# A cross-interaction network on one core: first tiles of three blocks by plain transfers, and a new order of fc's products, V2's spreading, loads of x and output transfers

## The chip, the core and the metric

The kernel runs on one core of a Trainium2 chip. A core has five engines, each with its own in-order queue of instructions: TensorE (PE in the profile; PEld is its loading of weights), VectorE (DVE), ScalarE (ACT), GpSimd (POOL) and SyncE (SP). Transfers between the chip's memory and the core's are issued by SP, ACT or POOL. The metric is the device time of one execution in microseconds (us), the median of several runs. Before the change it is 735.69 us, the median of three runs from 734.51 to 737.69.

## The reference

Inputs are x (1024 x 39 x 64: batch, fields F, embedding E), three weight matrices and the final layer. All is float32.

```python
def _cin_layer(Xk, X0, W, b):          # O = 64
    Wr = W.reshape(O, Hk, Fdim)
    return jnp.einsum('bhe,bfe,ohf->boe', Xk, X0, Wr) + b[None, :, None]
X0 = sparse_embedding; Xk = X0; outs = []
for W, b in ((W0, b0), (W1, b1), (W2, b2)):
    Xk = _cin_layer(Xk, X0, W, b)
    outs.append(Xk.sum(axis=-1))
return jnp.concatenate(outs, axis=-1) @ fc_w.T + fc_b
```

The last two layers are followed by nothing but sums and the final dot product, so their weights can be folded with fc_w. What is left per (batch, embedding) column is two quadratic forms of the 39 fields with 64 rows each: the first layer's, and one with W1 folded with "V2" (W2 folded with fc_w). They are multiplied with each other row by row, and summed.

## The kernel before, in words

**Work.** The 1024 x 64 columns are cut into 32 blocks of 2048 columns (`BLK`). The table `xd` in the chip's memory holds the fields as rows (39, and a row of ones): three buffers of two blocks each, filled by `load(n)`, a transfer of 1248 pieces of 256 bytes. A quadratic form needs the products of all pairs of fields. For blocks 0 to 3 and 30, 31 (the "whole" blocks) five tiles of 128 x 2048 (`rt[..][:, i]`, i = 0 to 4) are filled with rows of `xd` in five different orders (`label(i, row)`), so that the products of six pairs of tiles (`PAIRS`: (0,1), (0,2), (3,1), (3,2), (0,4), (3,4)), with one small product for two blocks, hold each pair of fields once. VectorE makes the products (`product`, L200), TensorE multiplies them with the weights `wa` (L551, four matmuls of 512 columns per product). The 26 blocks in between are done in another way (narrow lists, products at L736, matmuls at L763), which the change does not touch.

**Who fills the tiles.** `roll(n)` (L155) issues five indirect transfers from POOL, one per tile, each with a list of row numbers; `roll_small` fills two smaller tiles u and v. For block 0 the tiles are filled in two halves of 1024 columns from `xh`, two early copies of the first block (L370 to L376). Block n+2 uses block n's buffers: its transfers wait until the last product of block n that reads the tile. So blocks 0 to 3 are fetched while block 0 and 1 are computed.

**Start.** Before the first real matmul the weights have to be prepared, on TensorE with other engines in between (L254 to L500). In order: products without use (`spin`, L257, into a bank `idle` that nobody reads) keep TensorE busy. `turn` (L306) turns a row of fc_w into a column: a matmul with one contracted row and one output column. VectorE puts the column of fc's third part into `fc2` (L346). Four matmuls with `fc2` fold W2 (L386). `turn_twice` (L311, called at L394) turns fc's second part. VectorE transposes the folded W2 (`blocks`, L406). `spread_v2` (L420) doubles its rows, and VectorE masks it into `v2` (L433). `turn_w0` (L399) transposes W0 in seven pieces. Four matmuls with `v2` fold W1 (L467). VectorE (L480) and ScalarE (L444, L487, L490) put both into the table `both`, from which the pairs' weights are gathered (L508, L510), transposed (L527) and copied to `wa` (L528, L529). Then L551 begins.

**Order of the work after that.** It is written out: a list `steps`; `whole_step` multiplies step `at`, and `make` makes the product four steps ahead (`AHEAD`). Transfers stand where these functions issue them. On SP's queue are the row of ones for the second buffer (L349), the loads of x (L140), the rearranged weights `wn` (L700) and the fields for the finish (L793); on POOL's the rolls. At the end `y` (three rows of 256 results, L1081) leaves by SP's queue, and `yl` (the last 256, L1091) by ACT's.

```python
def turn(dst, row):
    nc.tensor.matmul(dst, row, one, start=True, stop=True)
...
def roll(n, tiles=range(NT), product=None):
    for i in tiles:
        k = n % 2 * NT + i
        gather_rows(tiles_of(n)[:, i], xd[n // 2 % NTAB][: FT if k < NT else 2 * FT], k, product)
```

Of the kernel before, what the change touches and what calls it, by code (L numbers as in the profile page):

```python
# [60 lines left out]
def label(i, row):  # L61
    if row < K:
        return (row % F + BASE[i] + STEP[i] * (row // F)) % F
    e = row - K
    if i == NT - 1 and e < ONLY:
        return F
    return 3 * e + (e >= ONLY) + (e > ONLY) + OFFSET[i]


# [45 lines left out]
def cin_kernel(ctx: ExitStack, tc: tile.TileContext, x, w0t, b0, w1, b1, w2, b2, fc_w, fc_b, out):  # L115
# [39 lines left out]
    def roll(n, tiles=range(NT), product=None):  # L155
        for i in tiles:
            k = n % 2 * NT + i
            gather_rows(tiles_of(n)[:, i], xd[n // 2 % NTAB][: FT if k < NT else 2 * FT], k, product)

    def roll_small(n):  # L160
        table = xd[n // 2 % NTAB].rearrange("f (t c) -> (f t) c", c=SUB)
        for k, dst in enumerate((ut, vt)):
            gather_rows(dst[n // 2 % 2], table, 2 * NT + k)
# [28 lines left out]
    unit = const.tile([128, 128], F32, name="unit")  # L192

    def product(n, c, cols=slice(0, BLK), p=None):
        if p is None:
            p = prods.tile([128, BLK], F32, name="p", tag="p")
        if c < NPAIR:
            i, k = PAIRS[c]
            r = tiles_of(n)
            nc.vector.tensor_tensor(p[:, cols], r[:, i, cols], r[:, k, cols], ALU.mult)  # L200
        else:
            nc.vector.tensor_tensor(p[:, 0:SUB], ut[n // 2 % 2], vt[n // 2 % 2], ALU.mult)
        return p

    prep = tc.tile_pool(name="prep", bufs=1)
    with prep as prep:
# [90 lines left out]
        for k, by in enumerate((*SHIFT, ROWS, *(ROWS + by for by in SHIFT[NK - 1 :]))):  # L297
            nc.gpsimd.memset(shift_of[:, k : k + 1], float(by))
        one = ones[0:1, 0, 0:1]

        def double(dst, src):
# [3 lines left out]
        def turn(dst, row):  # L305
            nc.tensor.matmul(dst, row, one, start=True, stop=True)  # L306
# [3 lines left out]

        def turn_twice(at, row, k):  # L311
            turn(small[:, at : at + 1], row[:, k].rearrange("p h s -> p (h s)"))

# [8 lines left out]
        first = pw[1][:, MM - 1 : MM]  # L322
        turn(first, fcrow2[:, 1].rearrange("p h s -> p (h s)"))
        spin(1, MM // 4)

# [44 lines left out]
        for k, cols in enumerate(halves):  # L370
            for i in range(4):
                gather_rows(rt[0][:, i, cols], xh[k], i)
                if k and i == 1:
                    load(1, nc.gpsimd)
        for k in (1, 0):
# [17 lines left out]

        turn_twice(6, fcrow2, 0)  # L394
        spin(1, 3 * MM // 8)

        def turn_w0(k):
# [5 lines left out]
            )  # L403

        for k in range(2):
            nc.vector.transpose(  # L406
                blocks[:, k].rearrange("p (f h) -> p f h", h=32),
                pv[k][:, 0:320].rearrange("p (h f) -> p f h", f=10),
            )
        nc.vector.tensor_scalar(v2v[:, 0, :, F - 32], mask, small[:, 6:7], None, ALU.mult)  # L410
        nc.vector.tensor_tensor(steps_at, steps_at, steps_by, ALU.mult)
# [16 lines left out]
        spread_v2(0, 0, 20)  # L428
        spread_v2(1, 1, 19)
        for k in range(7):  # L430
            turn_w0(k)
# [22 lines left out]
        roll_small(0)  # L454
        roll(1)
        for h in (0, H):
            nc.gpsimd.dma_start(b0s[h : h + H], b0.rearrange("(h o) -> h o", o=1))
        nc.gpsimd.dma_start(b1s, b1.rearrange("(h o) -> h o", o=1).to_broadcast([H, 2]))
        nc.gpsimd.dma_start(b2s, b2.rearrange("(h o) -> h o", o=1))
# [462 lines left out]
    for at, (n, c) in enumerate(steps[:3]):  # L922
        if at < 2:
            weight_rows(steps[3][1], slice(6 * at, 6 + 6 * at))
        product(n, c, halves[1], p[n, c])
    weight_rows(steps[4][1])
    n, c = steps[3]
# [15 lines left out]
    def whole_step(at, n, c):  # L943
        if at == NPAIR - 1:
            nc.scalar.copy(ones1, ones)
            fill_ones(1, nc.sync, ones1)
            for k in (2, 3):
                load(k)
        if (n, c) in ((0, NPAIR - 1), (2, 0)):
            load(2 * n + 4 - n // 2 * 2)  # L950
            load(2 * n + 5 - n // 2 * 2)
        quarters = range(BLK // MM)
# [40 lines left out]
    def make(at):  # L993
        step = steps[at]
        if len(step) == 2:
            n, c = step
            if NK < at <= NPAIR:
                weight_rows(c)
            p[n, c] = product(n, c)
            if c == NPAIR - 1 and n < 2:  # L1000
                rolls_due.append(lambda: roll(n + 2))
                if not n:
                    rolls_due.append(lambda: roll_small(2))
            if (n, c) == (2, NPAIR - 1):
                rolls_due.append(lambda: gather_slots(first_part, *range(7)))
            return
# [73 lines left out]
    nc.scalar.activation(y, py[0 : NY * 32, 0:YB], AF.Identity, bias=kfin)  # L1080
    nc.sync.dma_start(outv[0:NY], y[0 : NY * 32 : 32])  # L1081
    for lo, hi in ((0, done), (done, YB)):
# [6 lines left out]
        else:  # L1089
            nc.vector.tensor_scalar(yl[:, lo:hi], py, kfin[0:1], None, ALU.add)  # L1090
    nc.scalar.dma_start(outv[NY : NY + 1], yl)  # L1091

# [41 lines left out]
```

## Time and profile before

| | us |
|---|---|
| median of three runs (lowest, highest) | 735.69 (734.51, 737.69) |
| the profiled execution's own time | 737.69 |
| its span, from the first to the last instruction | 735.9 |
| TensorE busy (share of the span) | 728.6 (99%) |
| VectorE busy | 636.8 (87%) |
| POOL busy | 537.2 (73%) |
| ScalarE busy | 114.6 (16%) |
| bytes moved by all transfers | 153.56 MB, mean 209 GB/s |
| mean granted TensorE clock, share of full | 0.998 |

The profile shows one execution. Its own time is the highest of the three runs, and 1.79 us of it lie outside the span. In the chain of waits each row is a start, a length and what filled it; "issue" is time for which the profile shows no cause. In the timeline each row is a start, a length, engine, line, operation, and what is written from what; x4 says that four instructions stand in the row, and square brackets tell the idle time of the engine just before and who ended it. A float32 matmul is shown as two instructions. The profile's ends of matmuls are modelled.

### The profile page before, as it was taken

The numbers are of one execution on the slowest core, as the hardware profiler recorded it, in microseconds if no ns is written. First come the engines' busy times: TensorE is split into PE (matmuls) and PEld (weight loads), VectorE is DVE, ScalarE is ACT, GpSimd is POOL, SyncE is SP. The second block draws the span as 40 slices with busy tenths as digits, with TensorE's granted clock in tenths as the row PEclk, the third lists the DMA queues.
The fourth block names the chain that finished last, engine by engine and source line by source line (L and its number), as shares of the span: only waits on it lengthen the run. The fifth ranks groups of instructions, "written<-read, shape, count | busy, mean of one in ns | idle before, by whom it ended". The sixth has DMA issues, their size and how long they took to land.

```text
span 735.9 us, 13756 instructions
## 1 busy us (share of the span) xinstructions
PE 728.6 (99%) x5930; PEld 339.0 (46%) x5930; DVE 636.8 (87%) x558; ACT 114.6 (16%) x198; POOL 537.2 (73%) x292
## 2 busy tenths in 40 slices
PE   8999999999999999999999999999999999999998
PEld 5444444444444444444444444444444444444443
DVE  6997999688897988979888897988979888897996
ACT  3242210020200202011020200202011020200322
POOL 7758988649778696987869778696987869775200
PEclk9999999999999999999999999999999999999999
DMA  9889998843938558284673937558294673855600
GB/s 299 306 262 411 374 293 254 260 153 96 319 94 250 195 159 293 68 299 141 201 245 93 321 94 253 193 157 289 70 301 142 206 240 95 288 175 190 268 1 0
DMA packets 77363, 153.56 MB, mean 209 GB/s; under 512 B 43848, under 2 KB 43917, under 8 KB 73974
## 3 DMA queue, kind: packets, MB, share of 16 engines
q0 software_dynamic: 32304, 130.39, 50.0%
q1 hardware_dynamic: 43298, 20.30, 11.3%
q10 hardware_dynamic: 1700, 1.99, 0.9%
q8 instruction: 46, 0.75, 0.4%
q14 instruction: 15, 0.12, 0.1%
HBM read 150.54 MB, written 10.60 MB: 219 GB/s over the span
## 4 chain that ended last, share of the span: by engine, by line
PE 98%; another core or an unknown queue 0%; issue 0%; DVE 0%; ACT 0%; DVEq 0%; ACTq 0%
PE po L763 76%; PE po L551 17%; PE po L776 2%; PE po L571 1%; PE idle L259 1%; PE po L582 0%; PE pv L386 0%; PE pw L399 0%; DVE flat L480 0%; ACT both L487 0%; PE tr L527 0%; DVE g L827 0%; PE po L691 0%; DVE sums L859 0%
## 5 line engine op out<-in xcount | busy, mean ns | idle before, releaser
L763 PE MATMUL po<-p,wc 32*128 32x512 f32 x1300 | 561.9, 588 | 0.0
L763 PE MATMUL po<-p,wn 32*128 32x512 f32 x3900 | 561.7, 588 | 0.0
L719 POOL DMA_INDIRECT r<-xd,narrow x130 | 381.0, 2931 | 99.0 <-DVE p L736 66.7
L763 PEld LDWEIGHTS po<-p,wn 32*128 32x128 f32 x3900 | 260.7, 185 | 209.8 <-issue 209.6
L763 PEld LDWEIGHTS po<-p,wc 32*128 32x128 f32 x1300 | 239.4, 185 | 86.6 <-issue 82.1
L736 DVE TENSOR_TENSOR p<-r 128x2048 f32<-128x2048 f32 x78 | 176.1, 2283 | 8.2 <-PE po L763 7.8
L825 ACT ACTIVATE z<-po,columns 64x512 f32<-64x512 f32 x128 | 87.3, 682 | 544.2 <-PE po L763 504.0
L736 DVE TENSOR_TENSOR p<-r,u 128x2048 f32<-128x2048 f32 x52 | 118.7, 2282 | 15.5 <-DMA r<-xd,narrow 8.0
L551 PE MATMUL po<-p,wa 128*128 128x512 f32 x288 | 127.5, 600 | 1.8 <-ACT wa L528 1.8
L200 DVE TENSOR_TENSOR p<-r 128x2048 f32<-128x2048 f32 (+2 forms) x42 | 82.1, 1978 | 8.2 <-DMA r<-xd,lists 5.1
L551 PEld LDWEIGHTS po<-p,wa 128*128 128x128 f32 x288 | 54.3, 192 | 70.8 <-issue 64.1
L147 POOL DMA_INDIRECT r<-xd,lists x26 | 67.5, 2594 | 25.9 <-DVE p L736 11.6
L736 DVE TENSOR_TENSOR p<-r,v 128x2048 f32<-128x2048 f32 x26 | 59.7, 2296 | 25.7 <-PE po L763 25.7
L827 DVE SCALAR_TENSOR_TENSOR g<-po,b0s,z 64x512 f32<-64x512 f32 x76 | 56.9, 749 | 5.7 <-ACT z L825 3.5
L719 POOL DMA_INDIRECT v<-xd,narrow x26 | 37.2, 1431 | 7.9 <-issue 7.9
L827 DVE SCALAR_TENSOR_TENSOR pairs<-po,b0s,z 64x512 f32<-64x512 f32 x26 | 19.5, 749 | 23.9 <-ACT z L825 21.7
L719 POOL DMA_INDIRECT u<-xd,narrow x26 | 27.5, 1057 | 7.9 <-issue 4.0
L809 DVE TENSOR_REDUCE sums<-g 103x16 f32<-103x1024 f32 x26 | 31.3, 1205 | 0.0
L827 DVE SCALAR_TENSOR_TENSOR both<-po,b0s,z 64x512 f32<-64x512 f32 x26 | 19.5, 749 | 0.8
L820 ACT COPY g<-r 39x1024 f32<-39x1024 f32 x12 | 12.1, 1042 | 31.9 <-DVE sums L848 18.9
L730 DVE TENSOR_TENSOR p<-u,v 128x1024 f32<-128x1024 f32 x13 | 15.7, 1209 | 1.1 <-PE po L763 1.1
L809 DVE TENSOR_REDUCE sums<-both 103x16 f32<-103x1024 f32 x13 | 15.7, 1205 | 0.0
(140 smaller groups left out, 184.4 us busy)
## 6 DMA issues: line engine op xcount, KB each, us to landing
xd<-in_x SPq DMA_DIRECT2D x30, 312.0 KB
g<-xd SPq DMA_DIRECT2D x26, 156.0 KB
r<-xd,narrow POOLq DMA_INDIRECT x130
pairs<-xd SPq DMA_DIRECT2D x13, 156.0 KB
both<-xd SPq DMA_DIRECT2D x13, 156.0 KB
wn<-wc SPq DMA_DIRECT2D x12, 168.0 KB
w2s<-in_w ACTq DMA_DIRECT2D x1, 624.0 KB
w1s<-in_w ACTq DMA_DIRECT2D x1, 624.0 KB
```

Source lines behind the costliest of these rows:

```text
L147: work = nc.gpsimd.indirect_dma_start(dst, None, table, bass.IndirectOffsetOnAxis(ap=lists[:, k : k + 1], axis=0))
L200: nc.vector.tensor_tensor(p[:, cols], r[:, i, cols], r[:, k, cols], ALU.mult)
L551: nc.tensor.matmul(po[n][m], wa[:, c, side : side + 2 * H], p[:, bass.ts(m, MM)], start=n % 2 == 0 and c == 0, stop=n % 2 == 1 and c == NP ...
L719: work = nc.gpsimd.indirect_dma_start(slot(k, j), None, table, bass.IndirectOffsetOnAxis(ap=narrow[:, j : j + 1], axis=0),)
L730: done = nc.vector.tensor_tensor(p[:, 0:SUB], slot(k, LEFT), slot(k, RIGHT + NK), ALU.mult)
L736: done = nc.vector.tensor_tensor(p.rearrange("p (k c) -> p k c", k=NK), slots(k, many, NK, side), slot(k, one)[:, bass.ts(side, MM)].unsqu ...
L763: nc.tensor.matmul(po[2 * k + side][s], weights(c, s)[:, kind : kind + 2 * H], p[rows, bass.ts(u, MM)], start=begin, stop=last and u == le ...
L776: nc.tensor.matmul(po[2 * k + side][s][half : half + H], weights(LINEAR, s)[:, H : 2 * H], slot(k, NK)[rows, bass.ts(side, MM)], start=Fal ...
L809: nc.vector.tensor_reduce(sums[:, at : at + BB].rearrange("p (h s b) -> p h s b", h=2, s=2)[:, :, side], g[k, side, b].rearrange("p (h b e ...
L820: nc.scalar.copy(gt[H : H + F], tiles_of(n)[0:F, 0, bass.ts(m, SUB)])
L825: nc.scalar.activation(z[one], po[n][m][other], AF.Identity, bias=fc0s[other])
L827: return lambda: nc.vector.scalar_tensor_tensor(gt[0:H, at], po[n][m][one], b0s[one], z[one], ALU.add, ALU.mult)
```

## The change

It does eight things, all outside the repeated middle of the kernel.

- `turn_wide` takes the place of `turn_twice`, and does the turn of fc's third part as well: it multiplies with a row of 128 ones (`line`) instead of one, and so writes 128 equal columns, of which the last is used. Both turns now stand ahead of the fold of W2, followed by a spin of 64 columns (128 before).
- Behind the fold of W2 stands a spin of 128 columns (a turn and a spin of 192 before).
- Behind `spread_v2` stand two new spins of 160 columns, ahead of `turn_w0`.
- `load(1)` on POOL's queue moves ahead of the four second-half gathers of block 0 (it stood between the second and the third).
- Tiles 0 and 1 of blocks 1, 2 and 3 no longer come by POOL's indirect transfers. `roll_plain` writes them by plain transfers on SP's queue, one per run of rows whose numbers go up in equal steps: 13 transfers for the two tiles. For block 1 they wait for the product of block 0's second step, second half.
- `load(2)`, `load(3)` move from SP's queue (where they followed the row of ones) to POOL's, behind block 1's tiles.
- `load(4)`, `load(5)` move from SP's queue to POOL's, ahead of block 3's tiles.
- At the end `y` leaves by ACT's queue and `yl` by SP's.

```diff
+def stretches(i):
+    found, row = [], 0
+    while row < 128:
+        first, n, by = label(i, row), 1, 0
+        if row + 1 < 128 and label(i, row + 1) > first:
+            by = label(i, row + 1) - first
+            while row + n < 128 and label(i, row + n) - label(i, row + n - 1) == by:
+                n += 1
+        if n > 16 and not any(n % k == 0 for k in range(7, 17)):
+            n -= n % 13
+        found.append((row, n, first, by))
+        row += n
+    return found
...
+    def roll_plain(n, i, product=None):
+        table = xd[n // 2 % NTAB][n % 2 * FT : n % 2 * FT + FT]
+        for row, many, first, by in stretches(i):
+            src = table[first : first + (many - 1) * by + 1 : max(by, 1)]
+            behind(nc.sync.dma_start(tiles_of(n)[row : row + many, i], src), product)
...
-        def turn_twice(at, row, k):
-            turn(small[:, at : at + 1], row[:, k].rearrange("p h s -> p (h s)"))
+        def turn_wide(dst, k):
+            row = fcrow2[:, k].rearrange("p h s -> p (h s)")
+            nc.tensor.matmul(dst, row, line, start=True, stop=True)
...
         first = pw[1][:, MM - 1 : MM]
-        turn(first, fcrow2[:, 1].rearrange("p h s -> p (h s)"))
-        spin(1, MM // 4)
+        turn_wide(pw[1][:, MM - MM // 4 : MM], 1)
+        second = small[:, MM - 1 : MM]
+        turn_wide(small[:, MM - MM // 4 : MM], 0)
+        spin(1, MM // 8)
...
                 gather_rows(rt[0][:, i, cols], xh[k], i)
-                if k and i == 1:
-                    load(1, nc.gpsimd)
+            if not k:
+                load(1, nc.gpsimd)
...
-        turn_twice(6, fcrow2, 0)
-        spin(1, 3 * MM // 8)
...
+        spin(1, MM // 4)
...
         spread_v2(1, 1, 19)
+        spin(2, 5 * MM // 16)
...
-        roll(1)
+        roll(1, range(2, NT))
...
+            for k in (2, 3):
+                load(k, nc.gpsimd)
...
+        if at == 1:
+            for i in range(2):
+                roll_plain(1, i, made[n, c])
...
-            for k in (2, 3):
-                load(k)
-        if (n, c) in ((0, NPAIR - 1), (2, 0)):
-            load(2 * n + 4 - n // 2 * 2)
-            load(2 * n + 5 - n // 2 * 2)
+        if (n, c) == (2, 0):
+            load(6)
+            load(7)
...
-                rolls_due.append(lambda: roll(n + 2))
+                for i in range(2):
+                    rolls_due.append(lambda i=i: roll_plain(n + 2, i))
+                rolls_due.append(lambda: roll(n + 2, range(2, NT)))
...
+                    for k in (4, 5):
+                        rolls_due.append(lambda k=k: load(k, nc.gpsimd))
...
-    nc.sync.dma_start(outv[0:NY], y[0 : NY * 32 : 32])
...
-    nc.scalar.dma_start(outv[NY : NY + 1], yl)
+    nc.sync.dma_start(outv[NY : NY + 1], yl)
+    nc.scalar.dma_start(outv[0:NY], y[0 : NY * 32 : 32])
```

The order of VectorE's instructions is the same before and after; so is ScalarE's, but for its output transfer. The three engines whose rows move are shown below at the places on which the prediction rests.

TensorE at the start, before. `idle` is the spins' bank, `pw` and `small` take the turned rows, `pv` the folded W2 and then its doubled rows, `pt` and the last `pv` the folded W1.

```order
L259 MATMUL idle<-const-float32-1.0 128x128
L306 MATMUL pw<-ones,fcrow_107 128x1
L259 MATMUL idle<-const-float32-1.0 128x128
L386 MATMUL pv<-w2s,fc_108 64x320 x4
L306 MATMUL small<-ones,fcrow_107 128x1
L259 MATMUL idle<-const-float32-1.0 128x192
L420 MATMUL pv<-blocks,twice 128x20
L420 MATMUL pv<-blocks,twice 128x19
L399 MATMUL pw<-unit,w0s 128x117 x6
L399 MATMUL pw<-unit,w0s 64x117
L467 MATMUL pt<-w1s,v_75 128x320 x2
```

The same place after; the lines have other numbers there.

```order
L284 MATMUL idle<-const-float32-1.0 128x128
L339 MATMUL pw<-ones,fcrow_107 128x128
L339 MATMUL small<-ones,fcrow_107 128x128
L284 MATMUL idle<-const-float32-1.0 128x64
L415 MATMUL pv<-w2s,fc_108 64x320 x4
L284 MATMUL idle<-const-float32-1.0 128x128
L447 MATMUL pv<-blocks,twice 128x20
L447 MATMUL pv<-blocks,twice 128x19
L284 MATMUL idle<-const-float32-1.0 128x160 x2
L425 MATMUL pw<-unit,w0s 128x117 x6
L425 MATMUL pw<-unit,w0s 64x117
L497 MATMUL pt<-w1s,v_75 128x320 x2
```

The turn into `small` has moved ahead of the fold of W2, both turns are 128 columns wide, and two spins stand between the spreading and W0.

SP's queue before, from its first transfer to the rearranged weights. `xd` is the table of x in its three buffers, `r` the tiles.

```order
L376 DMA xd_68<-xh_72 39x1024
L376 DMA xd_68<-xh_71 39x1024
L349 DMA xd_69<-ones_95 16x2x128
L140 DMA xd_69<-in_x 1248x1x64 x2
L140 DMA xd_70<-in_x 1248x1x64 x2
L140 DMA xd_68<-in_x 1248x1x64 x2
L700 DMA wn<-wc 32x1344 x12
```

SP's queue after, from the same place to the first transfers of block 2.

```order
L405 DMA xd_68<-xh_72 39x1024
L405 DMA xd_68<-xh_71 39x1024
L179 DMA r_89<-xd_68 39x2048 x3
L179 DMA r_89<-xd_68 9x2048
L179 DMA r_89<-xd_68 2x2048
L179 DMA r_89<-xd_68 4x2048
L179 DMA r_89<-xd_68 35x2048
L179 DMA r_89<-xd_68 2x2048
L179 DMA r_89<-xd_68 26x2048
L179 DMA r_89<-xd_68 11x2048
L179 DMA r_89<-xd_68 39x2048
L179 DMA r_89<-xd_68 9x2048
```

Here follow one more run of two rows, the row of ones, 13 transfers each for blocks 2 and 3, the loads of the first buffer and the rearranged weights. Four of the six loads have left the queue.

POOL's queue before, from the first block's last tile to the first narrow gathers.

```order
L147 DMA r_88<-xd_68,lists 128x2048
L147 DMA u_90<-xd_68,lists 128x1024
L147 DMA v_92<-xd_68,lists 128x1024
L147 DMA r_89<-xd_68,lists 128x2048 x5
L457 DMA b0s<-in_b 64x1 x2
L458 DMA b1s<-in_b 128x1x1
L459 DMA b2s<-in_b 64x1
L460 DMA fcb<-in_fc_b 96x1
L349 DMA xd_70<-ones 16x2x128
L147 DMA r_88<-xd_69,lists 128x2048 x5
```

The same after.

```order
L162 DMA r_88<-xd_68,lists 128x2048
L162 DMA u_90<-xd_68,lists 128x1024
L162 DMA v_92<-xd_68,lists 128x1024
L162 DMA r_89<-xd_68,lists 128x2048 x3
L485 DMA b0s<-in_b 64x1 x2
L155 DMA xd_69<-in_x 1248x1x64 x2
L488 DMA b1s<-in_b 128x1x1
L489 DMA b2s<-in_b 64x1
L490 DMA fcb<-in_fc_b 96x1
L378 DMA xd_70<-ones 16x2x128
L162 DMA r_88<-xd_69,lists 128x2048 x3
```

Each block has three gathers where it had five, and the loads of the second buffer stand among the small loads of biases.

More of the change, by code (lines that the diff above doesn't have):

```diff
@@ L192, in cin_kernel @@
     unit = const.tile([128, 128], F32, name="unit")
+    made = {}
     def product(n, c, cols=slice(0, BLK), p=None):
@@ L199, in product @@
             r = tiles_of(n)
-            nc.vector.tensor_tensor(p[:, cols], r[:, i, cols], r[:, k, cols], ALU.mult)
+            made[n, c] = nc.vector.tensor_tensor(
+                p[:, cols], r[:, i, cols], r[:, k, cols], ALU.mult
+            )
         else:
@@ L299, in cin_kernel @@
         one = ones[0:1, 0, 0:1]
+        line = ones[0:1, 0, 0 : MM // 4]
         def double(dst, src):
@@ L409, in cin_kernel @@
             )
-        nc.vector.tensor_scalar(v2v[:, 0, :, F - 32], mask, small[:, 6:7], None, ALU.mult)
+        nc.vector.tensor_scalar(v2v[:, 0, :, F - 32], mask, second, None, ALU.mult)
         nc.vector.tensor_tensor(steps_at, steps_at, steps_by, ALU.mult)
```

## The prediction

> **What bounds the kernel now.** I read the page's first lines, then the chain of waits in order of time, then the timeline of the first 30 us and of the end, and last the granted clock in short windows. The page says that TensorE has work nearly all the time:
>
> ```profile
> PE 728.6 (99%) x5930; PEld 339.0 (46%) x5930; DVE 636.8 (87%) x558; ACT 114.6 (16%) x198; POOL 537.2 (73%) x292
> ```
>
> So a change that takes no work from TensorE can only gain where the chain is not made of the real matmuls (L551, L763). The chain shows where that is:
>
> ```profile
> 0.78 3.32 PE idle L259 x8
> 4.10 0.51 PE pw L306 x2
> 4.61 0.73 PE idle L259 x2
> 5.34 2.33 PE pv L386 x8
> 7.67 0.51 PE small L306 x2
> 8.18 0.94 PE idle L259 x2
> 9.12 0.55 PE pv L420 x4
> 9.67 1.57 PE pw L399 x7
> ...
> 16.48 3.08 another core or an unknown queue
> 19.56 0.25 ACT wa L528
> ...
> 19.86 2.08 PE po L551 x2
> ...
> 22.14 2.29 PE po L551 x4
> ...
> 24.54 6.87 PE po L551 x16
> ...
> 45.89 39.68 PE po L551 x92
> ...
> 730.45 0.02 issue
> ```
>
> The first real matmul starts at 19.86 and the last ends at 730.45; in between the chain is PE without a gap. That leaves three places: the 19.86 us before, a possible new gap in between, and the 735.9 - 730.45 = 5.45 us behind.
>
> Two things in the first 25 us need a look. First, TensorE's speed. L386's eight instructions took 2.33, and four of L467, also 320 columns each, took 2.21 at 11.02 and 1.32 at 13.07. The 896 columns of spins at 0.78 took 3.32 (3.7 ns a column), the 768 at 14.64 took 1.57 (2.04 ns).
>
> ```profile
> 11.02 2.21 PE L467 MATMUL pt<-w1s,v 128*128 128x320 f32 x4
> 13.07 1.32 PE L467 MATMUL pv<-w1s,v 128*128 128x320 f32 x4
> 14.64 1.57 PE L259 MATMUL idle<-const-float32-1.0 128*128 128x256 f32 x6
> 17.28 0.30 PE L527 MATMUL tr<-unit,pairs 128*128 128x128 f32 x1 [1.07 <-issue]
> ```
>
> So everything before some moment close to 13 ran at about half speed. After the idle stretch the clock falls again; here the windows show it:
>
> ```profile
> 20.00:21.00 1.00, 1.00 (x2) 0.48 (x3) 1.00 (x9) 0.34 (x2) 0.00 (x0) 0.50 1.01 397
> 23.00:24.00 1.00, 1.00 (x3) 0.46 (x3) 1.00 (x2) 0.00 (x0) 0.69 (x2) 0.92 0.91 385
> ```
>
> The granted clock was 0.50 from 20 to 23. Against 6.87 / 16 = 0.43 per instruction, the first six cost (2.08 - 0.86) + (2.29 - 1.72) = 1.79 us more. Second, ACT's copy at 19.56: by its row the transpose it waits for ended at 17.28 + 0.30 = 17.58, 1.98 us earlier, and the chain names an unknown queue. The profiled execution took 737.69, its span and 1.79 outside it, which is 2.00 above the median of 735.69. I take these 1.98 as peculiar to it: 737.69 - 1.98 = 735.71. From here on I count changes from the median.
>
> **The change part by part.** *fc's turns.* Both now stand ahead of L386. The second adds at least the 0.51 of the row at 4.10 there; 128 columns wide, it costs at most what a spin of 128 columns does, 0.73. Widening the first adds 0 to 0.22. The spin behind goes from 128 to 64 columns, 0 to 0.22 less. I take 0.6 more ahead of L386. Behind it the turn (0.51) goes and the spin shrinks from 0.94 (192 columns) to 0.73 (128): 0.72 less. Net for L420: -0.1. The cover is VectorE, which must finish transposing:
>
> ```profile
> 7.72 0.52 DVE L406 STREAM_TRANSPOSE blocks<-pv 128x320 f32<-128x320 f32 x1 [0.55 <-PE pv L386]
> ```
>
> It ends at 8.24, shifted by 0.6 at 8.84; L420 then starts at about 9.0, still behind it.
>
> *V2's spreading.* The two spins of 160 columns stand ahead of L399, and L467 waits in TensorE's queue behind them. At the slow speed a spin costs between 0.73 and 0.94, so two cost 1.67; at the fast speed 160 x 2.04 ns = 0.33 each, 0.65. No row shows work that would hide them: between L420 and L467 TensorE waited for nothing.
>
> *The clock.* Nothing else can pay for this. If the full speed comes before L399 instead of close to 13, L399 falls from 1.57 to about 0.79 and the first L467 pair from 2.21 to 1.32: -1.67. If it comes during L386, up to half of 2.33 goes too, -1.17; I take half of that, -0.6. For an early clock speak the rows: from 9.67 on TensorE streamed (1.57 + 2.21 us with no gap) and was fast by 13.07; before, the stretches of streaming were cut by two turns of one column, 0.51 each, that move almost nothing. The change fills just these. Against it: the 3.32 us of spins at the start did not raise the clock either. [...]
>
> Sum if the clock rises early: -0.1 + 0.65 - 1.67 - 0.6 = -1.7. If not: -0.1 + 1.67 = +1.57 up to L399; the first L467 pair is then late enough to run fast, which gives back 0.89: +0.7.
>
> What lies between L467 and L551 (VectorE's and ScalarE's making of the tables) keeps its order, so it shifts as a whole. The next that could be late is the first block's tiles; VectorE took their second halves only at 24.43. Their gathers stand on POOL on both sides of `load(1)` at 13.44, so moving it ahead of the first two makes these about 1.07 later, with some 10 us to spare.
>
> ```profile
> 13.44 1.07 POOL L140 DMA_DIRECT2D xd<-in_x  x1
> 24.43 2.35 DVE L200 TENSOR_TENSOR p<-r 128x1024 f32<-128x1024 f32 x2
> ```
>
> *Plain transfers and loads.* They change who waits for whom, not TensorE's work.
>
> ```profile
> 37.15 2.29 DVE L200 TENSOR_TENSOR p<-r 128x2048 f32<-128x2048 f32 x1 [0.39 <-DMA r<-xd,lists]
> 62.56 2.29 DVE L200 TENSOR_TENSOR p<-r 128x2048 f32<-128x2048 f32 x1 [4.68 <-DMA r<-xd,lists]
> L147 POOL DMA_INDIRECT r<-xd,lists x26 | 67.5, 2594 | 25.9 <-DVE p L736 11.6
> 39.55 13.71 SPq L140 DMA_DIRECT2D xd<-in_x  x6
> 87.58 9.50 SPq L700 DMA_DIRECT2D wn<-wc  x12
> ```
>
> Block 2's first product waited 4.68 for its tiles and was done at 64.85. TensorE needs it after 24 of block 1's matmuls, 48 of the 92 instructions of the row at 45.89: 45.89 + 48 x 0.431 = 66.6. So the wait was hidden, with 1.7 to spare. A start 1.7 earlier uses exactly that up. The change frees it: POOL loses two gathers of 2.59 per block and gains two loads of 1.07, and the tiles come by SP, which loses four of its six loads (13.71 x 4/6 = 9.1). No row has a plain transfer into these tiles; the nearest is `wn`'s, 12 in 9.50, 0.79 each. So I take 10.3 of SP for 13. Block 1's wait for the second half of block 0's second product, the end of the pair at 24.43, so 26.8; they are issued by 37.1. Queued behind on SP are the row of ones (at 39.15 before) and block 2's transfers, none of which the chain needs before 60. Block 1's first product, made at 37.15, may slip to 45.89 - 2.29 = 43.6 before TensorE waits. I put all this at 0, bounds -0 (there is no gap to win) and whatever exceeds 43.6.
>
> *The end.*
>
> ```profile
> 732.46 0.44 ACT L1088 ACTIVATE yl<-py,kfin 1x248 f32<-1x248 f32 x1
> 732.58 0.76 SPq L1081 DMA_DIRECT2D out_y<-y  x1
> 733.11 0.21 DVE L1090 TENSOR_SCALAR yl<-py,kfin 1x8 f32<-1x8 f32 x1 [0.45 <-PE py L1084]
> 733.40 0.27 ACTq L1091 DMA_DIRECT2D out_y<-yl  x1
> ```
>
> The last transfer was issued by 733.67. Now SP issues `yl` after 733.32 in about the same 0.27, and ACT `y` from 732.90 in 0.76, by 733.66. Both end together: 0, bounds -0.2 and +0.3.
>
> Total: 735.69 - 1.7 = **734.0**. With the bounds of the terms (-2.4 to -0.8 for an early clock) 733.3 to 734.9.
>
> **The rivals.** *The spins cost and the clock stays slow* (slower). Place: between L420 and L399. Price +0.7, bounds 0 to +1.57, so 736.4, or 735.7 to 737.3. It decides as soon as L399 still takes 1.57. For it: the spins at 0.78 raised nothing, and neither did L386. [...]
>
> *The second slow stretch goes too.* If the first L551 comes early enough that the clock does not fall ahead of it, the 1.79 at 20 to 24 are saved as well: 735.69 - 1.7 - 1.79 = 732.2, with the full L386 term 731.6. For it: the fall came just before 20, behind an idle stretch that an earlier start moves. Against: the wait between the spins' end at 16.2 and L551 has the same links as before.
>
> *Something else sets the start.* If ACT's release at 19.5 hangs on the transfers after all, an earlier L467 only makes a longer wait: 735.7. For it: the row names a queue.
>
> *The plain transfers are slow* (slower). If 13 take twice 10.3, block 1's first product slips from 37.15 to 26.8 + 20.6 + 2.3 = 49.7 at its end, 3.8 past 45.89; a like delay in block 2 or 3 adds: 739.5 and up. It decides at 43.6. Against: they have 16 us. [...]
>
> **How the numbers follow.** Forecast 0.42, slow spins 0.20, no second fall 0.20, start set elsewhere 0.12, slow transfers 0.06. The range 731.8 to 737.2 leaves out the slow transfers, half of "no second fall" and the upper edge of the spins, 0.2 in all. A measurement of this kernel can tell about 0.5%, 3.7 us, from no change: faster means below 732.0, slower above 739.4. Faster is over half of "no second fall" and the lower edge of the forecast, 0.17; slower the transfers and a little more, 0.07; the same 0.76.
>
> **What would show it.** Right: the four instructions of the first L467 pair take close to 1.3 and L399 under 1; the first real matmul starts near 16 to 18; from there the chain is PE alone; block 2's first product no longer waits. Wrong: L399 at 1.57 and spins of over 0.7 each; a wait of TensorE for a product between 20 and 110; a start at 19.9 again with a longer wait of ACT. A time below 731.5 or above 737.5 would say that a mechanism is missing here.

## The result and the profile after

The changed kernel takes **759.6 us** (median of six runs, 757.31 to 763.5), the kernel before beside it 735.5 (six runs, 734.51 to 740.15). The ratio is 1.032, 95% interval 1.029 to 1.035: slower by 3.2%, far outside the forecast range of 731.8 to 737.2. The profiled execution took 757.34, with a span of 755.6. It is among the shortest of its six, and the profiled one before (737.69, span 735.9) among the longest, so the two profiles differ by 19.7 us where the medians differ by 24.1.

The page of the changed kernel: TensorE's busy share and the chain of waits by engine and by line. (New lines: L179 is `roll_plain`, L223 the product, L581 the first real matmul, L793 the repeated middle, L730 `wn`, L155 the loads, L162 the gathers, L425 `turn_w0`, L415 the fold of W2, L497 the fold of W1.)

```profile
PE 735.0 (97%) x5934; PEld 341.5 (45%) x5934; DVE 636.6 (84%) x558; ACT 114.8 (15%) x198; POOL 519.9 (69%) x290
PE 87%; DMA 7%; POOL 2%; DVE 2%; SPq 1%; issue 1%; ACT 0%; DVEq 0%
PE po L793 74%; PE po L581 8%; DMA wn<-wc 3%; DMA xd<-in_x 3%; DMA r<-xd 2%; PE po L806 2%; POOL r L162 1%; SPq L730 1%; PE idle L284 1%; DVE p L223 1%; PE po L601 1%; DVE g L857 0%; PE pv L415 0%; POOL v L162 0%; PE po L612 0%
```

Before, the chain from 19.86 to 730.45 was TensorE alone. Now transfers stand in it. TensorE's timeline shows where; the single row below them is the profile before where the repeated middle begins, as L793 does after:

```profile
17.91 1.12 PE L581 MATMUL po<-p,wa 128*128 128x512 f32 x2
...
42.15 1.06 PE L612 MATMUL po<-u,wa 32*64 32x512 f32 x16
57.18 3.78 PE L581 MATMUL po<-p,wa 128*128 128x512 f32 x4 [13.97 <-DVE p L223]
...
81.38 19.12 PE L581 MATMUL po<-p,wa 128*128 128x512 f32 x44 [1.44 <-DVE p L223]
...
126.47 0.69 PE L793 MATMUL po<-p,wc 32*128 32x512 f32 x1
```

```profile
111.54 0.69 PE L763 MATMUL po<-p,wc 32*128 32x512 f32 x1
```

VectorE's row for block 1's first product, which the 13.97 wait for, and the granted clock behind it (the figure after the busy times):

```profile
54.84 2.29 DVE L223 TENSOR_TENSOR p<-r 128x2048 f32<-128x2048 f32 x1 [18.13 <-DMA r<-xd]
```

```profile
50.00:60.00 10.00, 2.82 (x4) 1.27 (x5) 5.13 (x13) 0.00 (x0) 4.08 (x4) 0.50 0.63 153
```

The sum of the loss, in shifts against the profile before: block 0 is done at 43.21 instead of 45.89 (-2.7); the wait ahead of block 1's first product costs 13.97; behind it the clock stands at half, and the first four instructions take 3.78 instead of 1.72 (+2.1); block 2's first product costs 1.44. That is +14.8, and L793 begins at 126.47 instead of 111.54: +14.9. The last real matmul ends at 750.22 instead of 730.45: +19.8. So 4.9 more are lost between, where `wn` comes late (the chain runs through its transfers until 132.16) and the granted clock is down once more (0.83 on average from 130 to 140).

SP's queue in the changed kernel: what was issued, from when, over how long.

```profile
25.63 17.60 SPq L179 DMA_DIRECT2D r<-xd  x13
...
53.55 36.96 SPq L179 DMA_DIRECT2D r<-xd  x26
91.34 14.59 SPq L155 DMA_DIRECT2D xd<-in_x  x2
106.09 15.80 SPq L730 DMA_DIRECT2D wn<-wc  x12
```

Block 1's 13 transfers were issued over 17.6 us, not 10.3. The first eight went out in 2.75 us, 0.34 each, less than half of the 0.79 that I took. The ninth was issued at 33.26, when the first had landed (33.24), the tenth at 37.09, when the second had (37.08), and so on: in this trace SP's queue never has more than eight of these transfers under way. The last was issued at 43.0 and landed at 54.4, by the trace's semaphore events. So it is not the issuing that is dear, but the landing.

The DMA view has packets, MB and the share of the 16 DMA engines' time for each queue (q0 POOL's, q1 SP's). Before, 60 to 85 us, while blocks 2 and 3 are fetched:

```profile
DMA packets 2067, 10.33 MB, mean 413 GB/s; under 512 B 645, under 2 KB 645, under 8 KB 998
...
q0 software_dynamic: 1599, 10.20, 98.7%
```

After, the same window:

```profile
DMA packets 1007, 6.09 MB, mean 244 GB/s; under 512 B 175, under 2 KB 175, under 8 KB 352
...
q0 software_dynamic: 655, 4.09, 68.0%
q1 hardware_dynamic: 351, 1.99, 33.4%
```

The DMA engines are as busy as before and move 59% of the bytes per us. While block 1 is fetched, 28 to 50 us, the engines were not full before, and they are nearly full after. First before, then after:

```profile
DMA packets 3441, 5.96 MB, mean 271 GB/s; under 512 B 2742, under 2 KB 2790, under 8 KB 2799
...
q0 software_dynamic: 934, 5.30, 65.7%
q1 hardware_dynamic: 2505, 0.64, 12.8%
```

```profile
DMA packets 1029, 5.35 MB, mean 243 GB/s; under 512 B 311, under 2 KB 328, under 8 KB 428
...
q0 software_dynamic: 666, 3.36, 58.0%
q1 hardware_dynamic: 361, 1.97, 34.5%
```

A row of 8 KB, by the trace's packet times between 28 and 50, took 354 ns in a gather before; now it takes 498 ns on SP's queue and 501 in a gather. The gathers are now as slow as SP's transfers.

### The profile page after: what moved, and what is told of

Same layout as the page of the kernel before. It is cut to its first block, busy times and chain, and to the rows that moved or that the text cites. A ratio compares the mean times of both kernels' runs of the same rounds, so it can differ in the third digit from the quotient of the medians.

```text
span 755.6 us, 13820 instructions
## 1 busy us (share of the span) xinstructions
PE 735.0 (97%) x5934; PEld 341.5 (45%) x5934; DVE 636.6 (84%) x558; ACT 114.8 (15%) x198; POOL 519.9 (69%) x290
## 4 chain that ended last, share of the span: by engine, by line
PE 87%; DMA 7%; POOL 2%; DVE 2%; SPq 1%; issue 1%; ACT 0%; DVEq 0%
PE po L793 74%; PE po L581 8%; DMA wn<-wc 3%; DMA xd<-in_x 3%; DMA r<-xd 2%; PE po L806 2%; POOL r L162 1%; SPq L730 1%; PE idle L284 1%; DVE p L223 1%; PE po L601 1%; DVE g L857 0%; PE pv L415 0%; POOL v L162 0%; PE po L612 0%
## 5 line engine op out<-in xcount | busy, mean ns | idle before, releaser
L793 PE MATMUL po<-p,wn 32*128 32x512 f32 x3900 | 566.2, 590 | 0.3 <-DMA wn<-wc 0.3
L793 PE MATMUL po<-p,wc 32*128 32x512 f32 x1300 | 562.1, 590 | 0.0
L749 POOL DMA_INDIRECT r<-xd,narrow x130 | 375.2, 2886 | 121.6 <-DVE p L766 67.7
L793 PEld LDWEIGHTS po<-p,wn 32*128 32x128 f32 x3900 | 262.2, 186 | 212.7 <-issue 209.9
L793 PEld LDWEIGHTS po<-p,wc 32*128 32x128 f32 x1300 | 239.1, 185 | 86.9 <-issue 80.6
L581 PE MATMUL po<-p,wa 128*128 128x512 f32 x288 | 128.5, 602 | 15.6 <-DVE p L223 15.4
L223 DVE TENSOR_TENSOR p<-r 128x2048 f32<-128x2048 f32 (+2 forms) x42 | 82.1, 1979 | 24.6 <-DMA r<-xd 18.8
L581 PEld LDWEIGHTS po<-p,wa 128*128 128x128 f32 x288 | 54.3, 193 | 85.8 <-issue 65.7
L162 POOL DMA_INDIRECT r<-xd,lists x20 | 52.2, 2609 | 28.4 <-DVE p L766 11.6
L839 DVE TENSOR_REDUCE sums<-pairs 103x16 f32<-103x1024 f32 x13 | 15.6, 1204 | 0.0
```

Of the source, the lines that this page charges most:

```text
L162: work = nc.gpsimd.indirect_dma_start(dst, None, table, bass.IndirectOffsetOnAxis(ap=lists[:, k : k + 1], axis=0))
L223: made[n, c] = nc.vector.tensor_tensor(p[:, cols], r[:, i, cols], r[:, k, cols], ALU.mult)
L581: nc.tensor.matmul(po[n][m], wa[:, c, side : side + 2 * H], p[:, bass.ts(m, MM)], start=n % 2 == 0 and c == 0, stop=n % 2 == 1 and c == NP ...
L749: work = nc.gpsimd.indirect_dma_start(slot(k, j), None, table, bass.IndirectOffsetOnAxis(ap=narrow[:, j : j + 1], axis=0),)
L793: nc.tensor.matmul(po[2 * k + side][s], weights(c, s)[:, kind : kind + 2 * H], p[rows, bass.ts(u, MM)], start=begin, stop=last and u == le ...
L839: nc.vector.tensor_reduce(sums[:, at : at + BB].rearrange("p (h s b) -> p h s b", h=2, s=2)[:, :, side], g[k, side, b].rearrange("p (h b e ...
```

## The experiments

The edits are given in short, not line for line.

### Which part of the change

**One: the start alone.**

```diff
 kernel before
+turn_wide twice, spin(1, 64); spin(1, 128); spin(2, 160); load(1) earlier
```

> The kernel before with the changed start alone: fc's wide turns, the spins of V2's spreading, load(1) earlier. No plain transfer, the loads and the output as before. Theory (the start gains by the second fall of the clock that goes): granted clock 1.00 between 20 and 25 instead of 0.50, L399's seven turns still near 1.4 to 1.6, 735.5 - 1.8 = 733.7 us. Rival one (the spins cost what they take and nothing pays): 736.4. Rival two (the start sets nothing): 735.5, with the first real matmul where the prepared weights let it start.

Measured: 734.91 against 734.64, ratio 0.9997 (0.998 to 1.0014). The start is worth nothing that can be measured, which is rival two's size. In its profiled execution TensorE did run fast early, the first row below falling from 1.57 to 0.86 and the second from 2.21 to 1.33, and the first real matmul came at 15.84:

```profile
9.80 0.86 PE L425 MATMUL pw<-unit,w0s 117*128 117x117 f32 x7
10.50 1.33 PE L495 MATMUL pt<-w1s,v 128*128 128x320 f32 x4
```

But then the chain leaves TensorE and goes through POOL's gathers of block 0's tiles:

```profile
11.70 1.07 POOL xd L155
...
14.38 7.59 DMA r<-xh,lists
...
23.44 4.53 PE po L579 x10
```

TensorE waits for the second halves of block 0's tiles and goes on at 23.44; the moved `load(1)` is a link of that chain with 1.07 us.

**Two: all but the plain transfers.**

```diff
-roll_plain of tiles 0 and 1
+roll(1), roll(n + 2): all five tiles by POOL
```

> The changed kernel with all five tiles of every block gathered by POOL, no plain transfer; the loads 2 to 5 stay on POOL's queue, start and end stay changed. Theory (the plain transfers are what is slow): 734 to 736 us, no gap of TensorE ahead of block 2, loads 2 and 3 landed some 10 us after their issue. Rival (the loads, put behind POOL's other work, land late by themselves): 750 or more, loads 2 and 3 still about 19 us from issue to landing.

Measured: 735.06, ratio 1.0006 (0.9988 to 1.0025). The theory holds: without plain transfers nothing is lost, and the moved loads cost nothing. Loads 2 and 3 landed 7 us after their issue; in the changed kernel the first of them took 19.4.

**Three: the plain transfers alone.**

```diff
 kernel before
+roll_plain of tiles 0 and 1 of blocks 1 to 3
```

> The kernel before with the plain transfers alone; start, loads and end as before, so that loads 2 to 7 stand on SP behind block 1's 13 transfers. Theory (the plain transfers are what is slow): 755 us or more, since the loads now leave only after these 13, and TensorE waits ahead of block 2. Rival (the loads on POOL are the cause): 735 to 737.

Measured: 764.64, ratio 1.041 (1.038 to 1.0435). The plain transfers are the whole loss; with the loads behind them on SP it is 5 us larger, and TensorE waits at both blocks:

```profile
56.55 22.34 PE L577 MATMUL po<-p,wa 128*128 128x512 f32 x48 [14.23 <-DVE lane_of L624]
91.58 21.86 PE L577 MATMUL po<-p,wa 128*128 128x512 f32 x44 [12.69 <-DVE p L223]
```

**Four: plain transfers in blocks 2 and 3 only. Ten: in block 1 only.**

```diff
 changed kernel                         changed kernel
-roll_plain(1, i)                      -roll_plain(n + 2, i)
+roll(1)                               +roll(n + 2)
```

> The changed kernel with block 1's tiles all gathered by POOL and plain transfers in blocks 2 and 3 alone. Theory (plain transfers slow whatever runs beside them): block 1's part of the loss goes and the part of blocks 2 and 3 stays; of the 19.8 us that were lost behind the start, between 5 and 15 stay, 742 to 752 us. Rival (only the first block's 13 are in the way, because they collide with the loads 2 and 3): 735 to 737.

> The changed kernel with plain transfers in block 1 alone; blocks 2 and 3 are gathered by POOL. In the changed kernel TensorE stood 13.97 us ahead of block 1's first product, whose last plain transfer was issued at 43.0 and landed at 54.4. Theory (the transfers of each block are late by themselves, and a wait at one block covers the wait at the next): the 14 us at block 1 stay whole, block 2 adds 1 to 2 because loads 2 and 3 land at 53 to 55: 735.5 + 14 = 749 to 751 us. Rival (the parts add up, and the run with plain transfers in blocks 2 and 3 has had 17 of the 24 us): 741 to 743.

Measured: 752.58 (ratio 1.024, 1.0212 to 1.0267) and 750.89 (1.021, 1.018 to 1.024). TensorE's only wait in the one and in the other:

```profile
81.09 20.86 PE L581 MATMUL po<-p,wa 128*128 128x512 f32 x44 [17.25 <-DVE p L223]
```

```profile
55.75 42.07 PE L581 MATMUL po<-p,wa 128*128 128x512 f32 x92 [13.12 <-DVE p L223]
```

The first came out just above what I expected, 742 to 752. Ten, within its 749 to 751, explains it: the parts do not add up. Either block's transfers cost 13 to 17 us alone; with both, the wait at block 1 covers nearly all of the wait at block 2 (1.44 in the changed kernel).

### Why these transfers are slow

**Five: each kind of transfer by itself.**

```diff
 kernel before, behind the output transfers
+64 rows x 8 KB, twice, to partitions 0-63 / 32-95 / 0-63 / 32-95, on SP; the same on POOL
+2 gathers; 13 plain transfers; 3 gathers and 13 plain transfers together
```

> The kernel before, with transfers added behind its output transfers, one step after the other, so that each kind is seen by itself: on SP's queue two copies of 64 rows of 8 KB to partitions 0 to 63, two to partitions 32 to 95, and both again; the same four steps on POOL's queue; then two tiles gathered by POOL; then the 13 plain transfers of two tiles; then three gathers and the 13 plain transfers together. The run's time is not compared; only the packets' mean times and the landing times count. In the changed kernel a plain packet of 8 KB took 521 ns, in the kernel before a gather's took 336 ns. Theory one (a copy is slow when its rows lie on few partitions that share a way into the memory): copies to partitions 0 to 63 have packets of 500 to 620 ns and copies to 32 to 95 of 310 to 360 ns, on SP's queue and on POOL's alike. Theory two (SP's queue itself is slow with such rows): about 520 ns for both places on SP, 310 to 360 for both on POOL. Theory three (the packets are not slow, but a run of 39 rows keeps only some of the 16 DMA engines busy): 310 to 360 ns for all four kinds, the 13 transfers alone take over 8 us because some engines are idle. [...]

The DMA view over four such steps, each 1.05 MB: SP to 0-63 (744.19 to 751.7), SP to 32-95 (751.7 to 757), then POOL to 0-63 (757.5 to 765.4) and POOL to 32-95 (765.4 to 770.9).

```profile
q1 hardware_dynamic: 160, 1.05, 63.2%
...
q1 hardware_dynamic: 160, 1.05, 54.8%
...
q0 software_dynamic: 160, 1.05, 61.8%
...
q0 software_dynamic: 160, 1.05, 50.8%
```

128 of the 160 packets are rows of 8 KB. A share times 16 engines times the window, over 128, gives 593 and 363 ns on SP, 610 and 349 on POOL; once under way the second kind takes 309. The other pass of each gave 622 and 400 on SP, 617 and 351 on POOL, so SP's second kind came out above the 310 to 360 that I expected. The rows, the bytes and the packets are the same (160 in each of the four, 32 of them under 512 B); only the partitions written differ. Theory one holds in the difference between the places, two falls, and three falls as the whole cause. The 13 plain transfers alone needed 15.5 us from the first issue (793.63) to the last landing (809.08), the two gathers, the same 2 MB, 9.0.

Theory one's reason, that the rows share a way into the memory, is shown by no run: what is measured is the difference between these two places, 593 against 363 ns on SP. No run tests tile 0's runs of 39 rows one by one.

**Eleven: the same bytes beside gathers.**

```diff
 kernel before, behind the output transfers, twice
+5 gathers; 3 gathers and 4 copies of 64 rows to 32-95; the same to 0-63; 3 gathers and the 13
```

> The kernel before, with four steps added behind its output transfers, one after the other, and the four once more: five tiles gathered by POOL; three gathered and four copies of 64 rows to partitions 32 to 95 on SP's queue; three gathered and the same four copies to partitions 0 to 63; three gathered and the 13 plain transfers. Each step moves 5 MB in rows of 8 KB; the run's time is not compared. Theory (the places that are written decide, and slow writes hold up the gathers that share the DMA engines): from the first issue to the last landing about 17 us, 15 to 18, 20 to 25 and 26. Rival one (a hardware queue beside POOL's is slow whatever it writes): 17, and 24 to 26 for all three mixed steps. Rival two (the places don't matter, the 13 transfers are slow because they keep few engines busy): 17, 15 to 18, 15 to 18 and 26.

Measured, first issue to last landing: 16.4, 15.1, 21.6 and 26.4 us; in the first round the last two took 21.9 and 26.3. The DMA view over the four windows of the second round (791.6, 808, 823.1, 844.9 to 871.4):

```profile
DMA packets 720, 5.24 MB, mean 320 GB/s; under 512 B 80, under 2 KB 80, under 8 KB 80
...
DMA packets 752, 5.24 MB, mean 347 GB/s; under 512 B 112, under 2 KB 112, under 8 KB 112
...
DMA packets 752, 5.24 MB, mean 241 GB/s; under 512 B 112, under 2 KB 112, under 8 KB 112
...
DMA packets 799, 5.24 MB, mean 198 GB/s; under 512 B 159, under 2 KB 159, under 8 KB 159
```

The theory holds, its numbers within a microsecond, and both rivals fall. SP's transfers beside POOL's cost nothing when they go to partitions 32 to 95 (15.1); on partitions 0 to 63 they cost 6.5 us more, and the gathers beside them slow down with them: while SP wrote, their 8 KB packets took, by the trace's packet times, 310 ns in the second step and 573 in the third. The 13 transfers cost another 4.8. What of it comes from their places, from the engines that carry each (an estimate of them stands under run seven), and from eight under way at most, these runs do not separate.

**Six and seven: tile 0 alone, as five transfers or as three.**

```diff
 changed kernel, roll(1, range(1, NT)), roll(n + 2, range(1, NT))
 seven:
-rows 0-38, 39-77, 78-116 by three transfers
+rows 0-116 by one, its source rows 0-38 three times over
```

> The changed kernel with only tile 0 by plain transfers (39, 39, 39, 9 and 2 rows, five instead of 13 a block); tile 1 is gathered by POOL with the other three. Theory one (runs of rows that lie on few partitions are moved at half speed): alone, tile 0's five were landed 8.8 us after the first was issued; beside four gathers that wait behind them this comes late by a part of the 19.8 us: 742 to 752 us. It is made to stand beside the next run, which moves the same rows. Rival (the number of transfers in SP's queue is what counts, eight may be under way): with five there is no queue, 735 to 737.

> The same as the run with tile 0 alone, but its three runs of 39 rows, which read the same 39 rows of the table, are one transfer of 117 rows (three transfers a block instead of five); the same rows go to the same places. Theory one (what counts is how many partitions are written at once): the rows of one transfer now lie on 117 partitions, the packets of 8 KB take 310 to 360 ns, tile 0 is landed within 5 us and no gap is left: 734 to 737 us. Rival one (a plain transfer's packets are slow beside gathers whatever its shape): the same time as the run with five transfers, within 2 us. Rival two (only the number of transfers counts): both at 735 to 737.

Measured: 741.44 (ratio 1.009, 1.006 to 1.012) and 773.05 (1.051, 1.047 to 1.055). Six fell just short of its range, and above its rival's: with five transfers a block TensorE still waits, 2.16 and 2.75 us ahead of block 2's products. Seven refuted every number that I wrote for it. TensorE's waits in it, and in the chain the wait for block 1's transfer:

```profile
58.46 23.15 PE L588 MATMUL po<-p,wa 128*128 128x512 f32 x48 [14.32 <-DVE lane_of L635]
92.38 21.53 PE L588 MATMUL po<-p,wa 128*128 128x512 f32 x44 [10.77 <-DVE p L230]
```

```profile
26.56 28.30 DMA r<-xd
```

The rest of its loss stands further on in the chain: a load behind these transfers on SP's queue (43.51 us from 74.30) and `wn` behind that, until 145.4.

The wide transfer's 8 KB packets were quick once most gathers had ended (313 ns between 45 and 50), as theory one has it. But there were few of them: between 45 and 55, 58 in 10 us, under two engines' work. In the trace of the changed kernel a run of 39 rows raises its semaphore 14 times (three of block 1's four), one of 35 rows 8, of 26 14, of 11 12, of 9 10, of 2 3; here the transfer of three times 39 rows raised it only 4 times. One of them comes with the issue (the first transfer of the changed kernel, issued at 25.63, at 26.13). No view names a packet's engine. If the others are one for each engine that carries a part, which is my estimate from these counts, I had built a transfer that three engines carry alone; 58 packets of 313 ns in 10 us, 1.8 under way at a time, agree with it. By that estimate seven does not test the places; what it shows is that quick packets do not make a quick transfer, 28.30 us for 117 rows.

### What follows from it

**Eight: `wn` on another queue.**

```diff
-nc.sync.dma_start(wn[...], wc[...])
+nc.scalar.dma_start(wn[...], wc[...])
```

> The changed kernel with wn's 12 transfers issued on ACT's queue instead of SP's, so that they no longer stand behind the plain transfers of blocks 2 and 3 and the loads 6 and 7. Theory (of the time lost behind the start, 16.8 us are lost ahead of and at block 2's first products, and 4.9 at the first use of wn, because SP's queue is late): the second part goes, 759.6 - 4.9 = 754.7, at least 753. Rival (wn is late because the DMA engines are full, not because of SP's order): 758 to 760.

Measured: 761.09 (ratio 1.035, 1.032 to 1.039). The time is the rival's, to a microsecond; its reason is not shown. (The expectation names block 2 for the first part of the loss; it is block 1's first product, as above.) The wait for `wn` did go: its transfers landed 3 us earlier than in the changed kernel's profile, at 128.96, and L793 began at 132.32 without waiting for them. But they held ScalarE's own work behind them, and TensorE waited for a product in their place. In this execution it also stood longer at block 2, 4.69 against 1.44:

```profile
83.03 20.82 PE L581 MATMUL po<-p,wa 128*128 128x512 f32 x44 [4.69 <-DVE p L223]
...
128.34 3.70 PE L581 MATMUL po<-p,wa 128*128 128x512 f32 x8 [1.88 <-DVE p L223]
```

```profile
105.82 15.83 ACTq L730 DMA_DIRECT2D wn<-wc  x12
121.69 1.99 ACT L850 COPY g<-r 39x1024 f32<-39x1024 f32 x2 [15.90 <-DMA wn<-wc]
```

SP's order did play a part in the changed kernel: there `wc` was ready at 102.44, and SP sent loads until 105.93 and `wn` from 106.09. Moving `wn` to ACT exchanged one wait for others; how much full DMA engines add stays open.

**Nine: plain transfers in blocks 2 and 3, the gathers held until they have landed.**

```diff
+roll_behind(n + 2): the gathers of tiles 2, 3, 4 wait for the block's 13 plain transfers
```

> Plain transfers in blocks 2 and 3 alone, as in the run at 752.6, but POOL's gathers of tiles 2, 3 and 4 of these blocks wait until the block's 13 plain transfers have landed. Theory (two things make block 2's first product late: the packets at half speed, and that tiles 0 and 1, which are needed first, share the DMA engines with all that POOL queues behind them): alone, the 13 were landed 15.4 us after the first issue, so from 49.1 by 64.5, where TensorE waited in that run from 63.8 to 81.1: a wait of 2 to 4 us is left, 736 to 740 us. Rival (the plain transfers take as long without company): 750 or more.

Measured: 752.76 (ratio 1.024, 1.021 to 1.027), no gain over run four. That is the rival's number, but not for its reason: block 2's 13 landed at 64.84, 15.8 us after the first issue, as I had reckoned, and the first wait shrank from 17.25 to 3.98. But the next product was late instead:

```profile
67.60 6.27 PE L597 MATMUL po<-p,wa 128*128 128x512 f32 x8 [3.98 <-DVE p L239]
...
83.80 18.74 PE L597 MATMUL po<-p,wa 128*128 128x512 f32 x36 [9.93 <-DVE p L239]
```

```profile
49.06 20.83 SPq L179 DMA_DIRECT2D r<-xd  x26
```

SP sent block 3's 13 straight behind block 2's (58.53 to 69.9), and tile 2's gather, issued at 65.80, landed 15.6 us later beside them. My sum left out block 3. This order only moved the wait; no other order was tried.

## Why the prediction was wrong

**Where it failed.** The step "Plain transfers and loads. They change who waits for whom, not TensorE's work", with its term of 0. I priced the issue (0.79 each from `wn`'s row, 10.3 for 13) and asked only when SP would be done. The landing was priced nowhere. It took 28.8 us from the first issue to the last landing, against the 16.8 that were to be had (26.8 to 43.6). Runs five and eleven show the cause in kind: a packet took 593 ns to partitions 0 to 63 and 363 to 32 to 95 (run five, SP), and a gather's packets took 573 beside writes to the first and 310 beside writes to the second (run eleven). The bound "whatever exceeds 43.6" was right, the size under it was not looked for: 13.97 at block 1, and with the half clock and the late `wn` behind it some 20 in all.

**What the profile before would have told.** The windows that I quoted for the clock end with the DMA engines' share and GB/s: "1.01 397" and "0.91 385". The DMA view of 60 to 85 us says 98.7% and 413 GB/s; between 28 and 50, where block 1 is fetched, some 79% and 271. The fetching of the tiles was as good as a second bound of the later stage and not far from one in the earlier, and a change from one way of fetching to another was to be costed in DMA time. `wn`'s transfers were the right row too, read for the wrong number: 12 runs of 32 rows of 5376 bytes, whose packets took 351 ns, 15 bytes per ns, where a gather's 8192 bytes took 336 over the whole execution, 24 per ns.

**The rival "plain transfers are slow"** named the place (block 1's first product), the condition (landed after 43.6) and the sign, and had 0.06. Its size, a doubling, would have been 3.8 us; the transfers took nearly three times as long. It should have been the forecast, or close to it.

**The other steps.** *fc's turns and spins:* L420's successor began at 8.86, for 9.0 forecast. Right. *The clock:* in the changed kernel's profile TensorE stayed slow, L425 took 1.57; in run one it was fast, 0.86. The clock records of the two traces begin only at 12.93 (before) and 13.25 (the changed kernel), with 1.00, so for the slow stretch ahead of that the times of the matmuls are all that is shown. Across the profiles either start shows either speed. The old start in run three, and the new one in run four:

```profile
5.14 1.38 PE L413 MATMUL pv<-w2s,fc 128*64 128x320 f32 x8
...
7.61 0.92 PE L423 MATMUL pw<-unit,w0s 117*128 117x117 f32 x7
```

```profile
5.79 2.40 PE L415 MATMUL pv<-w2s,fc 128*64 128x320 f32 x8
...
10.62 1.57 PE L425 MATMUL pw<-unit,w0s 117*128 117x117 f32 x7
```

Of the thirteen profiles four have the old start, and in three of them W0's transposing ran at the fast speed (0.92, against 1.63 in the fourth); nine have the new one, and in five of them it did (0.86 to 0.92, against 1.57). So the argument that streaming without gaps brings the clock up is not borne out; what sets the moment stays open. The -1.7 was also counted from the one late profile of the old start, while the median from which it was subtracted may well hold mostly early ones. And running fast early brought little forward: the first matmul that waited for the second halves of block 0's tiles came at 22.33 and 22.50 with the old start (runs three and eleven), at 22.61 to 23.81 with the new (one, two, eight, nine). *The second slow stretch* was gone in run one (granted 1.00 between 20 and 25), as the rival had it, and the median did not move. *"Something else sets the start"* is what run one shows, though not by the link that I named: where TensorE is fast early, the gathers of block 0's tiles are last. *`load(1)`: "some 10 us to spare"* held only where TensorE was fast late; in run one it lies on the chain. *The 1.98 us "peculiar" to the profiled execution:* such a wait came again with the old start in run five, 2.39, and in run eleven, 1.61; it belongs to some executions, and its cause stays open.

```profile
17.57 1.93 PE L577 MATMUL po<-p,wa 128*128 128x512 f32 x2 [2.39 <-issue]
```

*The loads on POOL:* 0 by run two, and beside the slow transfers a gain of 5 (764.64 against 759.6). *The end:* 755.6 - 750.22 = 5.4, before 5.45. Right: the two transfers are issued by 753.18 and 753.43.

```profile
752.36 0.82 ACTq L1126 DMA_DIRECT2D out_y<-y  x1
...
753.17 0.26 SPq L1125 DMA_DIRECT2D out_y<-yl  x1
```

No run points to a version that beats both kernels: without the plain transfers the rest of the change measures 1.0006.

## What to carry to other kernels

Price a transfer that you move by its landing, not its issue (28.8 us here, where the issue had been priced at 10.3), from a run with its own rows, the partitions that it writes (593 against 363 ns a packet in run five) and what shares the DMA engines at that time (a gather's packets took 354 ns before and 501 beside the plain transfers). Where the DMA share stands near 1, as it did here at 98.7%, the transfers can be a bound of the stage even if TensorE shows no wait. Replacing gathers of 128 rows by runs of neighbouring rows cut the rate of all transfers together to 59% here. A gain sought where the chain has no gap can only show as a loss.

## What the runs showed of the hardware

- The same 64 rows of 8 KB took 593 to 622 ns each to partitions 0 to 63 and 349 to 400 to 32 to 95, on SP's queue and on POOL's (run five). Beside such writes to 0 to 63 a gather's packets took 573 ns, beside the 13 transfers 515, beside writes to 32 to 95 310 (run eleven, second round).
- A plain transfer on SP's queue raised its semaphore 14 times for 39 rows, 8 for 35, 3 for 2 (the changed kernel), and 4 times for three times 39; the last took 28.3 us for 0.96 MB (run seven).
- POOL's load of x moved its 312 KB as 78 packets of 4 KB, SP's as 1248 of 256 bytes (both kernels).
- After an idle stretch of 14 us TensorE ran at a granted clock of 0.50 again, at a cost of about 2 us (the changed kernel).
